# Layer 0's first and last blocks over three PSUM banks, its table cleared in pieces, and layer 3's output bias added by GpSimd

## The chip, the cores and the metric

The kernel runs on one core of one Trainium2 chip, in one launch. The metric is the device time in microseconds of that core. A profiled execution gives the trace; lines such as L187 are lines of the kernel before the change.

## The reference, cut to what matters

Four layers in a row turn `x` of 4 images, 128 channels and 48 x 48 pixels into an output of the same shape. All is float32.

- Layer 0, for each image: a layer norm over each pixel's channels, an input projection to 2 x 256 channels, a depthwise 3 x 3 convolution with silu, four selective scans (two directions by rows, two by columns) with 16 states over 2304 pixels, their sum, a norm over 256 channels, a gate, an output projection, and the image itself added.
- Layer 1: a deformable 3 x 3 convolution. A plain convolution of layer 0's output gives 27 offset channels; every output pixel then reads nine places of the image with bilinear weights. Pixels outside the image count as zero.
- Layer 2: eight linear-attention blocks, and then 64 experts that each take 8 tokens of every image.
- Layer 3: one causal attention with 4 heads of 32 channels over each image's 2304 tokens, and again 64 experts. Its output projection is `t = t + (out @ out_w.T + out_b)`, and the experts follow.

## The kernel before

**Layer 0** works image by image. Three steps matter here, and for images 1 to 3 (the first) and 0 to 2 (the last) they are slipped in among the scans of another image; only image 0's start and image 3's end stand alone.

- `before(im, j)`: six blocks of 384 pixels. A block is a list of ten steps: fetch `xb`, three transposes (L247), copy to `xt` (L251), statistics (L207 to L210, the last one a power on GpSimd), normalise (L214), three transposes back (L257), scale and shift into `xn` (L261) with a DMA of it to memory (L262), and two projections (L266), each copied into a padded image (L269).
- `convolve(d, r)`: 24 groups of nine matmuls over the padded image (L187), each emptied by ScalarE into `u_hw` (L294). Then silu (L302), and `prepare` for the first scan, whose first DMA writes `rows` (L372); the scans read `rows` back into `rB`, one DMA a step (L500).
- `post(im)` after an image's last scan: six blocks `after(im, j)` of 18 steps (fetch `yb`, `xn`, `xb`; transposes L634, copies L641, statistics, L214, transposes L648, L653, the gate L663 and L674, silu with its table load L677 and the reload L678, L681, projection L686, sum L691, transposes L697, L701 and the DMA L702 to `tok`), and then six blocks `offsets(im, j)`: two groups of nine matmuls (L187 with `l_woT`), L747, transposes L754, L760, and a DMA. After the last block four DMAs copy `tok` into `table` (L709). Layer 1 gathers from `table` (L949).

`merged(lists, lag)` puts lists of steps into one order, list i starting i x lag steps later. Image 0's blocks use lag 10, the last blocks lag 18; both are the length of a list, so that blocks follow one another. Every one of these steps takes its PSUM tile from the pool `pf`, which has one bank:

```
def psum(*shape):
    return pf.tile(list(shape), F32, name="pf", tag="pf")
```

PSUM's eight banks go to `ps` (two, for the scans' transposes), `pf` (one), `pu` (one, for `prepare`), `yp` (three) and `b0` (one).

`table` has a border of zeros. At the start GpSimd sets the whole of `y` (128 x 4608) to zero (L169) and ten DMAs copy it over the table (L173), 21.3 MB.

TensorE, ScalarE, VectorE and GpSimd take their instructions in program order (`manual_schedule`). The queue of SyncE (SP), which issues these DMAs, isn't in that list; its order is the scheduler's.

**Layer 3** runs scores (L2061), exponentials (L2069), masks on GpSimd (L2072) and weighted sums (L2090) block by block, while the row maxima of the next block (L2007, L2016, L2017) and the preparation of later ones (`prepare`: L1946, transposes L1958, projections L1964 and L1982) are slipped in between. `output` projects a finished block and adds it to the tokens `T`:

```
for g in range(G3):
    nc.tensor.matmul(pp[:, g, :], oT[:, bass.ts(g, P)], oT_w, start=True, stop=False)
    nc.tensor.matmul(pp[:, g, :], env.ones_row, o_b, start=False, stop=True)
dst = im.T[:, j * G3 : (j + 1) * G3, :]
nc.vector.tensor_add(dst, dst, pp)
```

These are L2041, L2042 and L2044; 24 blocks with three pairs each. `o_b` holds the bias with the values' bias folded in (L2145, L2146).

Of the kernel before, what the change touches and what calls it, by code (L numbers as in the profile page):

```python
# [23 lines left out]
P = 128  # L24
NB = 4
C = 128
# [73 lines left out]
]  # L100
NPI = len(PIECES)
TPC = CH // P
CT = 512
HBUF = 3
HB = BLK // 2
# [2 lines left out]
def _layer0(ctx, env, dr, io, table, offs):  # L108
# [16 lines left out]
    def load(name, shape):  # L125
        t = cp.tile(shape, F32, name=name)
        nc.sync.dma_start(t, io[name])
        return t

    def psum(*shape):  # L130
        return pf.tile(list(shape), F32, name="pf", tag="pf")

    ln_g = load("l0_ln_g", [P, 1])
# [27 lines left out]
    for pad in pads:  # L161
        nc.gpsimd.memset(pad, 0.0)


    u_hw = wp.tile([P, ND, L], F32, name="u_hw")
    u_wh = wp.tile([P, ND, L], F32, name="u_wh")
    y = wp.tile([P, ND, L], F32, name="y")
    zero = y.rearrange("p d f -> p (d f)")
    nc.gpsimd.memset(zero, 0.0)  # L169
    flat = table.rearrange("r c -> (r c)").rearrange("(p f) -> p f", p=P)  # L170
    for i in range(0, flat.shape[1], ND * L):
        w = min(ND * L, flat.shape[1] - i)
        nc.sync.dma_start(flat[:, i : i + w], zero[:, :w])  # L173


# [136 lines left out]

    def merged(lists, lag):

        out = []
        for t in range(max(i * lag + len(a) for i, a in enumerate(lists))):
            for i, a in enumerate(lists):
                if 0 <= t - i * lag < len(a):
                    out.append(a[t - i * lag])
        return out  # L320

    def chained(lists):
# [8 lines left out]
        return out  # L331

    def pre(im):
        items = merged([before(im, j) for j in range(NBLK)], 10)
        return items + chained([convolve(d, r) for r in range(L // HB) for d in range(ND)]) + [activate]

    class Piece:
# [279 lines left out]
    def after(im, j):  # L617

        cols = bass.ts(j, BLK)
        t = {}  # L620

        def fetch():
            t["yb"] = sp.tile([P, ND, BLK], F32, name="yb", bufs=1)
            nc.sync.dma_start(t["yb"], im.y[:, :, cols])
            t["xn"] = sp.tile([P, BLK], F32, name="xn")
            nc.sync.dma_start(t["xn"], im.xn[:, cols])
            t["xb"] = sp.tile([P, BLK], F32, name="xb")
            nc.sync.dma_start(t["xb"], io["x"][im.b][:, cols])

        def turn_y(g0, g1):  # L630
            t["pt"] = pt = psum(P, g1 - g0, DI)
            for g in range(g0, g1):
                for d in range(ND):
                    nc.tensor.transpose(  # L634
                        pt[:, g - g0, bass.ts(d, P)], t["yb"][:, d, bass.ts(g, P)], ident
                    )

        def turned(g0, g1):
            if g0 == 0:
                t["yt"] = sp.tile([P, G3, DI], F32, name="yt", bufs=1)  # L640
            nc.scalar.copy(t["yt"][:, g0:g1, :], t.pop("pt"))  # L641
            if g1 == G3:
                t["first"], t["second"] = standardise(t["yt"])

        def back_y(d):
            t["pt"] = pt = psum(P, BLK)
            for g in range(G3):
                nc.tensor.transpose(pt[:, bass.ts(g, P)], t["yt"][:, g, bass.ts(d, P)], ident)  # L648

        def normed(d):  # L650
            if d == 0:
                t["yn"] = sp.tile([P, ND, BLK], F32, name="yn", bufs=1)
            nc.scalar.activation(  # L653
                t["yn"][:, d, :],
                t.pop("pt"),
                AF.Identity,
                bias=ob[:, d : d + 1],
                scale=og[:, d : d + 1],
            )

        def gate(d):
            t["pz"] = psum(P, BLK)
            nc.tensor.matmul(  # L663
                t["pz"],
                ipT[:, DI + d * P : DI + (d + 1) * P],
                t["xn"],
                start=True,
                stop=True,
            )

        def gate_out(d):
            if d == 0:
                t["z"] = sp.tile([P, ND, BLK], F32, name="yt", bufs=1)
            nc.scalar.copy(t["z"][:, d, :], t.pop("pz"))  # L674

        def silu():
            nc.scalar.activation(t["z"], t["z"], AF.Silu)  # L677
            nc.scalar.preload_act_table_set(EXP_LN)  # L678

        def gated():  # L680
            nc.vector.tensor_mul(t["yn"], t["yn"], t["z"])  # L681
# [12 lines left out]
        def to_table():  # L694
            t["pt"] = pt = psum(P, G3, P)
            for g in range(G3):
                nc.tensor.transpose(pt[:, g, :], t["xb"][:, bass.ts(g, P)], ident)  # L697

        def out():
            xt = sp.tile([P, G3, C], F32, name="xt")  # L700
            nc.scalar.copy(xt, t.pop("pt"))  # L701
            nc.sync.dma_start(im.tok[cols, :].rearrange("(g p) c -> p g c", p=P), xt)  # L702
            if j == NBLK - 1:
                tb = table[im.b * TROWS : (im.b + 1) * TROWS, :].rearrange(
                    "(y x) (q c) -> y x q c", x=TW, c=C
                )
# [27 lines left out]

    def offsets(im, j):
        t = {}

        def third(i, n):
            if n == 0:
                t["pp"] = psum(NOFF, HB)  # L740
            taps(t["pp"], woT, pads[0], 2 * j + i, 3 * n, 3 * n + 3)

        def rows(i):
            if i == 0:
                t["fo"] = sp.tile([P, G3, DI], F32, name="yt", bufs=1)
                t["fo"] = t["fo"].rearrange("p g c -> p (g c)")[:NOFF, :BLK]
            nc.scalar.activation(  # L747
                t["fo"][:, bass.ts(i, HB)], t.pop("pp"), AF.Identity, bias=bo
            )

        def turn():
            t["pt"] = pt = psum(P, G3, NOFF)
# [21 lines left out]
        ]  # L774

    def post(im):
        return merged([after(im, j) for j in range(NBLK)], 18) + chained(
            [offsets(im, j) for j in range(NBLK)]
        )
# [21 lines left out]
                self.done += 1  # L801

    with tc.manual_schedule(engines=ORDERED):
        for s in pre(images[0]) + prepare(pieces[0], None):
            s()
        for g in range(3):
            do(row, g)
# [13 lines left out]
        for g in range(len(pieces) * NS + 2):  # L821
# [2 lines left out]
            if n == 0 and i + 1 < len(pieces):  # L824
                lanes["next"] = Lane(prepare(pieces[i + 1], pieces[i]), 3 * (NS - 3))
            if (p, n) == (0, 5) and b < NB:
                items = post(images[b - 1]) if b else []
                cols = [lambda d=d, j=j: columns(d, j) for j in range(NCH) for d in range(ND)]
                gap = len(items) // len(cols)
                for q, c in enumerate(cols):  # L830
# [33 lines left out]
            do(scan, g, 1)  # L864
        for d in range(ND):
            collect(pieces[-1], d)
        for s in post(images[-1]):
            s()

# [1003 lines left out]
def _layer3(ctx, env, io, T):  # L1873
# [26 lines left out]
    v_b = load("l3_v_b", [P, 1])  # L1900
    oT_w = load("l3_owT", [P, C])
    o_b = load("l3_ob", [1, C])
    later = load("l3_later", [P, P])

    spread = [cp.tile([P, G3, P], F32, name=f"spread{i}") for i in range(NP3)]
# [31 lines left out]
    def prepare(im, j):  # L1937
# [15 lines left out]
                )  # L1953

        def turn():
            pt = psum(P, BLK)
            for g in range(G3):
                nc.tensor.transpose(pt[:, bass.ts(g, P)], t["xn"][:, g, :], ident)  # L1958
# [78 lines left out]
    def output(im, j, oT):  # L2037
        def project():
            pp = psum(P, G3, C)
            for g in range(G3):  # L2040
                nc.tensor.matmul(pp[:, g, :], oT[:, bass.ts(g, P)], oT_w, start=True, stop=False)  # L2041
                nc.tensor.matmul(pp[:, g, :], env.ones_row, o_b, start=False, stop=True)  # L2042
            dst = im.T[:, j * G3 : (j + 1) * G3, :]
            nc.vector.tensor_add(dst, dst, pp)  # L2044

# [299 lines left out]
```

## Time and profile before

| what | us |
|---|---|
| median of 3 runs | 12765.19 (12760.49 to 12773.71) |
| profiled execution | 12769.64, of which the span is 12767.5 |
| image 0's six blocks, first transpose to first convolution | 10.44 to 102.58 |
| image 0's 24 convolution groups | 102.58 to 193.16, the start of the last L294 |
| first `rows` DMA of the scans | 204.46 |
| last image: `y` written, first transposes of its blocks | 5214.98, 5225.55 |
| last image: first offset convolution, copy of the last offsets | 5354.59, 5404.73 |
| layer 1's first gather | 5421.81 |
| layer 3: first statistics, start of the last sum into `T` | 11025.19, 12564.3 |

Over the whole span TensorE is busy for 10986.9 us (86%), VectorE 8483.4 (66%), ScalarE 6895.6 (54%), GpSimd 4394.0 (34%). In the timeline a line gives the start, the duration, the engine, the line of the kernel, the operation with what it writes and reads, and in brackets how long the engine sat idle before it and what ended that. A matmul in float32 is listed as two passes, so nine matmuls are x18.

### The profile page before, as it was taken

The numbers are of one execution on the slowest core, as the hardware profiler recorded it, in microseconds if no ns is written. First come the engines' busy times: TensorE is split into PE (matmuls) and PEld (weight loads), VectorE is DVE, ScalarE is ACT, GpSimd is POOL, SyncE is SP. The second block draws the span as 40 slices with busy tenths as digits, with TensorE's granted clock in tenths as the row PEclk, the third lists the DMA queues.
The fourth block names the chain that finished last, engine by engine and source line by source line (L and its number), as shares of the span: only waits on it lengthen the run. The fifth ranks groups of instructions, "written<-read, shape, count | busy, mean of one in ns | idle before, by whom it ended". The sixth has DMA issues, their size and how long they took to land.

```text
span 12767.5 us, 192717 instructions
## 1 busy us (share of the span) xinstructions
PE 10986.9 (86%) x71150; PEld 8409.7 (66%) x71150; DVE 8483.4 (66%) x15484; ACT 6895.6 (54%) x13189; POOL 4394.0 (34%) x4775
## 2 busy tenths in 40 slices
PE   6879778877887787588879999999999998799997
PEld 4667666766676666378757777777777776333333
DVE  4998889888988899444455656656566565445444
ACT  3777777777777677411125555555556565232222
POOL 1443333333333334166633333333333332100001
PEclk9999999999999999799979999999999999799998
DMA  2221222122222222266610000000000001200003
GB/s 103 67 70 65 76 79 69 65 77 79 69 65 75 82 66 68 65 174 174 177 44 2 4 3 4 4 2 4 2 4 4 1 1 43 84 6 7 7 8 124
DMA packets 307846, 677.50 MB, mean 53 GB/s; under 512 B 39108, under 2 KB 128984, under 8 KB 304864
## 3 DMA queue, kind: packets, MB, share of 16 engines
q1 hardware_dynamic: 254032, 493.49, 12.0%
q0 software_dynamic: 51840, 169.91, 4.6%
q8 instruction: 571, 9.36, 0.3%
q14 instruction: 363, 2.97, 0.1%
q10 hardware_dynamic: 1040, 1.77, 0.0%
HBM read 602.63 MB, written 71.85 MB: 53 GB/s over the span
## 4 chain that ended last, share of the span: by engine, by line
PE 43%; DVE 7%; ACT 3%; issue 1%; DMA 1%; POOL 1%; another core or an unknown queue 0%; SPq 0%; ACTq 0%; DVEq 0%; POOLq 0%
PE psum L1425 4%; PE pt L962 4%; PE psum L1417 4%; PE pc L1311 3%; PE psum L1361 3%; PE scT L2061 3%; PE sc L2007 3%; PE out L2090 3%; PE psum L1331 2%; PE psum L1171 2%; PE psum L1172 2%; PE psum L1105 2%; PE psum L1249 1%; PE psum L1350 1%; DVE mx L1334 1%
## 5 line engine op out<-in xcount | busy, mean ns | idle before, releaser
L565 ACT ACTIVATE hs<-ps,bct 128x256 f32<-128x256 f32 x4608 | 1858.3, 475 | 1171.1 <-PE ps L559 1121.1
L559 PE MATMUL ps<-ident,h 128*128 128x128 f32 x9216 | 1499.4, 295 | 776.2 <-DVE h L545 602.1
L559 PEld LDWEIGHTS ps<-ident,h 128*128 128x128 f32 x9216 | 1087.4, 149 | 1158.4 <-DVE h L545 708.5
L573 PE MATMUL yp<-ident,hs 128*128 128x128 f32 x9216 | 1409.1, 289 | 28.6 <-ACT ys L588 28.6
L505 ACT ACTIVATE dA<-delta,l_Al 128x768 f32<-128x768 f32 x1536 | 1388.4, 936 | 0.3
L512 POOL TENSOR_TENSOR h<-du,rB 128x512 f32<-128x512 f32 x768 | 1079.0, 1405 | 768.9 <-PE ps L559 691.0
L573 PEld LDWEIGHTS yp<-ident,hs 128*128 128x128 f32 x9216 | 1161.6, 151 | 83.0 <-ACT ys L588 57.7
L545 DVE TENSOR_TENSOR_SCAN h<-dA,h 128x256 f32<-128x256 f32 (+1 forms) x1024 | 1084.2, 1059 | 27.3
L545 DVE TENSOR_TENSOR_SCAN h<-dA,carry,h 128x768 f32<-128x768 f32 x512 | 1026.7, 2005 | 10.5 <-ACT dA L505 10.5
L1165 POOL TENSOR_TENSOR T<-T,bias 128x384 f32<-128x384 f32 x384 | 384.3, 1001 | 1558.5 <-DVE fn L1093 1518.3
L487 POOL TENSOR_SCALAR_AFFINE_SELECT dB<-bct 128x512 f32<-128x512 f32 x768 | 749.5, 976 | 379.2 <-PE b L519 236.3
L2069 ACT ACTIVATE pT<-scT 128x768 f32<-128x768 f32 (+2 forms) x504 | 378.1, 750 | 897.3 <-PE scT L2061 897.1
L519 PE MATMUL b<-dB,duT 128*128 128x128 f32 x6144 | 827.5, 278 | 0.8 <-ACT duT L445 0.8
L545 DVE TENSOR_TENSOR_SCAN h<-dA,carry,b 128x512 f32<-128x512 f32 x512 | 645.6, 1261 | 269.6 <-PE b L519 250.7
L962 PE MATMUL pt<-ident,gw 128*128 128x128 f32 x5184 | 677.1, 292 | 167.7 <-DVE gw L956 139.0
L949 POOL DMA_INDIRECT g<-table,idx x648 | 656.9, 1014 | 412.4 <-DVE gw L956 179.4
L962 PEld LDWEIGHTS pt<-ident,gw 128*128 128x128 f32 x5184 | 642.2, 205 | 197.3 <-DVE gw L956 133.5
L519 PEld LDWEIGHTS b<-dB,duT 128*128 128x128 f32 x6144 | 767.9, 196 | 2.4 <-POOL h L512 1.2
L956 DVE TENSOR_TENSOR gw<-g,wq 128x512 f32<-128x512 f32 x648 | 425.7, 692 | 494.1 <-PE pt L962 420.6
L552 POOL COPY carry<-h 128x2 f32<-128x2 f32 x512 | 97.9, 191 | 1784.4 <-DVE h L545 1714.5
L2017 DVE TENSOR_REDUCE mx<-sc 128x2 f32<-128x1024 f32 (+3 forms) x400 | 428.4, 1071 | 364.5 <-PE sc L2007 359.4
L516 DVE TENSOR_TENSOR h<-du,rB 128x512 f32<-128x512 f32 x768 | 629.3, 819 | 3.7 <-DMA rB<-rows 3.6
(345 smaller groups left out, 22964.7 us busy)
## 6 DMA issues: line engine op xcount, KB each, us to landing
rB<-rows SPq DMA_DIRECT2D x768, 384.0 KB
w<-f_w SPq DMA_DIRECT2D x64, 1024.0 KB
table<-y SPq DMA_DIRECT2D x9, 2304.0 KB
table<-tok SPq DMA_DIRECT2D x16, 1152.0 KB
g<-table,idx POOLq DMA_INDIRECT x648
xb<-x SPq DMA_DIRECT2D x48, 192.0 KB
xn<-xn SPq DMA_DIRECT2D x48, 192.0 KB
yd<-y SPq DMA_DIRECT2D x4, 2304.0 KB
```

The lines of the kernel that those rows point to most:

```text
L487: nc.gpsimd.affine_select(out=x.dB[n], in_=x.bc[:, m0 : m0 + CT // P, n : n + 1].to_broadcast([P, CT // P, P]), pattern=[[0, CT // P], [1, ...
L505: nc.scalar.activation(dA, x.delta[:, d, :], AF.Exp, scale=A[:, d, x.k, n : n + 1])
L512: nc.gpsimd.tensor_mul(h[:, 1, own], x.du[:, 1, own], x.rB[n][:, own])
L516: nc.vector.tensor_mul(x.h[n][:, :, own], x.du[:, :, own], b)
L519: nc.tensor.matmul(b0[:, bass.ts(m, P)], x.duT[:, m, :], x.dB[n][:, m, :], start=True, stop=True,)
L545: nc.vector.tensor_tensor_scan(h, da, b, initial=first, op0=ALU.mult, op1=ALU.add)
L559: nc.tensor.transpose(tt[:, m, bass.ts(d, P)], x.h[n][:, d, bass.ts(2 * q + m, P)], ident)
L565: nc.scalar.activation(hs, tt[:, m, :], AF.Copy, scale=x.bc[:, 2 * q + m, NS + n : NS + n + 1])
L573: nc.tensor.matmul(yp[:, q, (2 * d + m) * P : (2 * d + m + 1) * P], hs[:, bass.ts(d, P)], ident, is_transpose=True, start=n == 0 and m == ...
L949: nc.gpsimd.indirect_dma_start(out=g, out_offset=None, in_=table, in_offset=bass.IndirectOffsetOnAxis(ap=idx[:, j : j + 1], axis=0),)
L962: nc.tensor.matmul(pt[:, t - t0, :], gw[:, q, :], ident, start=q == 0, stop=q == 3)
L1417: nc.tensor.matmul(pg, y.w["w1"][:, bass.ts(f, P)], t["uT"], start=True, stop=True)
```

## The change

The pieces are independent of one another.

1. While `banks` is filled, `psum` hands out three banks in turn, `pf` and the two of `ps`. It is filled for image 0's start and for the last image's end. Image 0's blocks then start every 3 steps instead of every 10.
2. The last image's blocks start every 6 steps instead of every 18, its offset blocks start at step 23 and then every 9 steps, and take their PSUM tile from `pu`. Their SBUF tiles come from buffers of the scans (`h`, `dA0`, `dA1`, `rB`, `xd`).
3. A tile of zeros of 128 x 256 takes the place of the zeroed `y`; 163 DMAs of 128 KB (the last one smaller) take the place of ten. Their calls stand in the list of steps that goes along with image 0's scans, between the six transposing copies of `columns`.
4. In layer 3 the bias row is spread over 128 partitions once (one matmul, one copy), GpSimd adds it to a block's tokens when the block is prepared, after it was normalised, and the 72 ones-row matmuls go.

```diff
+ZW = 256
...
+    banks = []
+
     def psum(*shape):
+        if banks:
+            banks.append(banks.pop(0))
+            pool, name = banks[-1]
+            return pool.tile(list(shape), F32, name=name, tag=name)
         return pf.tile(list(shape), F32, name="pf", tag="pf")
...
-    zero = y.rearrange("p d f -> p (d f)")
+    zero = cp.tile([P, ZW], F32, name="zero")
     nc.gpsimd.memset(zero, 0.0)
     flat = table.rearrange("r c -> (r c)").rearrange("(p f) -> p f", p=P)
-    for i in range(0, flat.shape[1], ND * L):
-        w = min(ND * L, flat.shape[1] - i)
+
+    def clear(i):
+        w = min(ZW, flat.shape[1] - i)
         nc.sync.dma_start(flat[:, i : i + w], zero[:, :w])
...
     def merged(lists, lag):
+        starts = lag if isinstance(lag, list) else [i * lag for i in range(len(lists))]
...
     def pre(im):
-        items = merged([before(im, j) for j in range(NBLK)], 10)
+        items = merged([before(im, j) for j in range(NBLK)], 3 if banks else 10)
...
         def fetch():
-            t["yb"] = sp.tile([P, ND, BLK], F32, name="yb", bufs=1)
+            if banks:
+                t["yb"] = sp.tile([P, ND, CH], F32, name="h", bufs=HBUF)[:, :, :BLK]
+                t["xn"] = sp.tile([P, CH], F32, name="dA0")[:, :BLK]
+                t["xb"] = sp.tile([P, CH], F32, name="rB", bufs=3)[:, :BLK]
+            else:
+                t["yb"] = sp.tile([P, ND, BLK], F32, name="yb", bufs=1)
...
-                t["yn"] = sp.tile([P, ND, BLK], F32, name="yn", bufs=1)
+                if banks:
+                    t["yn"] = sp.tile([P, CH], F32, name="dA1")
...
-                t["z"] = sp.tile([P, ND, BLK], F32, name="yt", bufs=1)
+                t["z"] = sp.tile([P, ND, BLK], F32, name="yb" if banks else "yt", bufs=1)
...
     def offsets(im, j):
+        def own(*shape):
+            return pu.tile(list(shape), F32, name="pu", tag="pu") if banks else psum(*shape)
...
     def post(im):
+        if banks:
+            lists = [f(im, j) for f in (after, offsets) for j in range(NBLK)]
+            starts = [6 * j for j in range(NBLK)]
+            starts += [9 * j + 23 for j in range(NBLK)]
+            return merged(lists, starts)
...
     with tc.manual_schedule(engines=ORDERED):
-        for s in pre(images[0]) + prepare(pieces[0], None):
+        free = [(pf, "pf"), (ps, "ps"), (ps, "ps")]
+        banks += free
+        for s in pre(images[0]):
+            s()
+        del banks[:]
+        for s in prepare(pieces[0], None):
             s()
...
-                items = post(images[b - 1]) if b else []
+                if b:
+                    items = post(images[b - 1])
+                else:
+                    items = [lambda i=i: clear(i) for i in range(0, flat.shape[1], ZW)]
...
+        banks += free
         for s in post(images[-1]):
             s()
...
+    bias = cp.tile([P, 1, C], F32, name="bias")
...
         def turn():
+            own = im.T[:, j * G3 : (j + 1) * G3, :]
+            nc.gpsimd.tensor_add(own, own, bias.to_broadcast([P, G3, C]))
             pt = psum(P, BLK)
...
-                nc.tensor.matmul(pp[:, g, :], oT[:, bass.ts(g, P)], oT_w, start=True, stop=False)
-                nc.tensor.matmul(pp[:, g, :], env.ones_row, o_b, start=False, stop=True)
+                nc.tensor.matmul(pp[:, g, :], oT[:, bass.ts(g, P)], oT_w, start=True, stop=True)
...
+        pr = psum(P, C)
+        nc.tensor.matmul(pr, env.ones_row, o_b, start=True, stop=True)
+        nc.scalar.copy(bias[:, 0, :], pr)
         run(normed(images[0]) + prepare(images[0], 0))
```

More of the change, by code (lines that the diff above doesn't have):

```diff
@@ L313, in merged @@
     def merged(lists, lag):
+        starts = lag if isinstance(lag, list) else [i * lag for i in range(len(lists))]
         out = []
[L316 to L319, printed above, removed]
+        for t in range(max(i + len(a) for i, a in zip(starts, lists))):
+            for i, a in zip(starts, lists):
+                if 0 <= t - i < len(a):
+                    out.append(a[t - i])
         return out
@@ L622, in fetch @@
         def fetch():
-            t["yb"] = sp.tile([P, ND, BLK], F32, name="yb", bufs=1)
+            if banks:
[4 more added lines that the diff above has]
+                t["yb"] = sp.tile([P, ND, BLK], F32, name="yb", bufs=1)
+                t["xn"] = sp.tile([P, BLK], F32, name="xn")
+                t["xb"] = sp.tile([P, BLK], F32, name="xb")
             nc.sync.dma_start(t["yb"], im.y[:, :, cols])
-            t["xn"] = sp.tile([P, BLK], F32, name="xn")
             nc.sync.dma_start(t["xn"], im.xn[:, cols])
-            t["xb"] = sp.tile([P, BLK], F32, name="xb")
             nc.sync.dma_start(t["xb"], io["x"][im.b][:, cols])
@@ L651, in normed @@
             if d == 0:
-                t["yn"] = sp.tile([P, ND, BLK], F32, name="yn", bufs=1)
+                if banks:
+                    t["yn"] = sp.tile([P, CH], F32, name="dA1")
+                    t["yn"] = t["yn"].rearrange("p (d f) -> p d f", d=ND)
+                else:
+                    t["yn"] = sp.tile([P, ND, BLK], F32, name="yn", bufs=1)
             nc.scalar.activation(
@@ L736, in offsets @@
         t = {}
+        def own(*shape):
+            return pu.tile(list(shape), F32, name="pu", tag="pu") if banks else psum(*shape)
         def third(i, n):
             if n == 0:
-                t["pp"] = psum(NOFF, HB)
+                t["pp"] = own(NOFF, HB)
             taps(t["pp"], woT, pads[0], 2 * j + i, 3 * n, 3 * n + 3)
@@ L744, in rows @@
             if i == 0:
-                t["fo"] = sp.tile([P, G3, DI], F32, name="yt", bufs=1)
-                t["fo"] = t["fo"].rearrange("p g c -> p (g c)")[:NOFF, :BLK]
+                if banks:
+                    t["fo"] = sp.tile([NR + 2 * NS, CH], F32, name="xd", bufs=1)
+                else:
+                    t["fo"] = sp.tile([P, G3, DI], F32, name="yt", bufs=1)
+                    t["fo"] = t["fo"].rearrange("p g c -> p (g c)")
+                t["fo"] = t["fo"][:NOFF, :BLK]
             nc.scalar.activation(
@@ L751, in turn @@
         def turn():
-            t["pt"] = pt = psum(P, G3, NOFF)
+            t["pt"] = pt = own(P, G3, NOFF)
             for g in range(G3):
@@ L776, in post @@
     def post(im):
+        if banks:
+            lists = [f(im, j) for f in (after, offsets) for j in range(NBLK)]
+            starts = [6 * j for j in range(NBLK)]
+            starts += [9 * j + 23 for j in range(NBLK)]
+            return merged(lists, starts)
         return merged([after(im, j) for j in range(NBLK)], 18) + chained(
@@ L826, in _layer0 @@
             if (p, n) == (0, 5) and b < NB:
-                items = post(images[b - 1]) if b else []
+                if b:
+                    items = post(images[b - 1])
+                else:
+                    items = [lambda i=i: clear(i) for i in range(0, flat.shape[1], ZW)]
                 cols = [lambda d=d, j=j: columns(d, j) for j in range(NCH) for d in range(ND)]
```

## The prediction

> **What bounds the kernel now.** I read the page's forty slices first, then busy time by stage, then the timeline of the stages that the change touches, and last the waits.
>
> ```profile
> PEclk9999999999999999799979999999999999799998
> ```
>
> The clock granted to TensorE has three 7s. The first, slice 17, is layer 0's end. Now the stages: image 0's blocks, its convolution, the last image's blocks, its offset convolution, and layer 3 after its start.
>
> ```profile
> core 0: us, PE busy (x) PEld busy (x) DVE busy (x) ACT busy (x) POOL busy (x), PEclk, DMA share, GB/s
> 10.00:102.00 92.00, 30.62 (x60) 12.31 (x60) 22.47 (x87) 6.90 (x12) 5.13 (x6) 1.00 0.63 258
> 103.00:193.00 90.00, 78.16 (x432) 71.22 (x431) 0.00 (x0) 9.69 (x23) 0.00 (x0) 1.00 0.00 1
> 5225.00:5354.00 129.00, 65.00 (x138) 27.85 (x138) 27.82 (x72) 42.45 (x60) 8.16 (x12) 0.51 0.13 35
> 5355.00:5405.00 50.00, 41.68 (x234) 24.01 (x232) 1.47 (x6) 4.95 (x12) 0.00 (x0) 0.95 0.36 103
> 11140.00:12565.00 1425.00, 1309.00 (x6206) 509.22 (x6205) 672.98 (x1122) 431.10 (x618) 65.79 (x139) 0.93 0.03 7
> ```
>
> In the two block stages no engine is busy for more than half the time: they are chains through one PSUM bank, and the latency of the chain ends last. Layer 3 is TensorE's: 1309 of 1425 us. The timeline shows the front's two losses, a stall and a pause for each convolution:
>
> ```profile
> 37.33 0.91 PE L257 MATMUL pf<-ident,xt 128*128 128x128 f32 x3 [3.62 <-DVE xt L214]
> 64.72 0.67 ACT L261 ACTIVATE xn<-pf,l_ln_b,l_ln_g 128x384 f32<-128x384 f32 x1 [30.46 <-DMA xn<-xn]
> ...
> 112.13 3.19 PE L187 MATMUL pf<-pad,diag 128*128 128x192 f32 x18 [0.51 <-ACT u_hw L294]
> 115.36 0.42 ACT L294 ACTIVATE u_hw<-pf,l_cb 128x192 f32<-128x192 f32 x1 [3.28 <-PE pf L187]
> 115.83 3.19 PE L187 MATMUL pf<-pad,diag 128*128 128x192 f32 x18 [0.51 <-ACT u_hw L294]
> ```
>
> L261 of the third block needs a buffer whose write to `xn` stands behind 21 MB of zeros for the table; after the transposes it would have started at 38.3, so 26.4 us are lost. And every convolution waits 0.51 us for the one bank to be emptied. In layer 3 the output projection alternates weights with the bias row:
>
> ```profile
> 11639.99 0.49 PE L2041 MATMUL ps<-l_owT,sums 128*128 128x128 f32 x2
> 11640.41 0.48 PE L2042 MATMUL ps<-l_ob,ones_row 1*128 1x128 f32 x2
> 11640.83 0.49 PE L2041 MATMUL ps<-l_owT,sums 128*128 128x128 f32 x2
> 11642.60 0.55 DVE L2044 TENSOR_TENSOR T<-T,ps 128x384 f32<-128x384 f32 x1 [1.26 <-PE ps L2042]
> ```
>
> From start to start a pair takes 0.42 us, the bias as much as the projection.
>
> **The change, part by part.** The sum is made against the profiled execution, 12769.64 us (span 12767.5); it lies 4.45 above the median 12765.19, inside the runs' own spread of 13 us.
>
> *Image 0's blocks.* Before, six blocks of 10.8 us (10.44 to 22.11) and the 26.4 us stall put the first convolution at 102.6. Changed, a block starts every 3 steps and three banks rotate. TensorE's queue then repeats: projection, next block's transposes, second projection, previous block's back-transposes. At the durations of this stage (L266 1.65, L247 0.90, L257 0.91) that is 5.1 us, and once in each round TensorE waits for L261 (0.67 and the two hand-overs, 0.8). The round is 5.9 us. VectorE needs less: three pairs of statistics 1.5, two small steps with GpSimd's power 1.3, L214 0.9, two pad copies 1.1, hand-overs, near 5.3. The first block's back-transposes end at 16.7 as now (VectorE's 18 `diag` products until 12.9 still go ahead), the second's at 22.6, the sixth's at 22.6 + 4 x 5.9 = 46.2, and L261 with two projections brings 51. Gain 51.5. If fetches and the two `xn` buffers stretch the round to 8 us it is 43; if TensorE warms up and VectorE's 5.3 sets the round, 54.
>
> *Its convolution.* 24 groups back to back: 24 x 3.19 and 2.1 for the first, cold one (5.27 at 102.58) are 78.7, against 90.6. Gain 12. L294 (0.42) is hidden under the next group's 3.19. Convolutions end at 130, and the first row transfer of the scans is due 11.3 us later (193.2 to 204.5 now), at 141.
>
> *The clears.* The text puts them among the scans, but SP's queue is not kept in program order: in the built changed kernel all 163 stand before the first `rows` write, 29 between the fetches and `xn` writes of image 0, then 134 in a row. So they don't do what their place says; what hides them is the convolution. From the last `xn` write, 47, to 141 there are 94 us, 0.70 us for each of 134. No 128x256 store is in the trace. The nearest row is the load of `l_opT`, also 128x256: issued at 6.31, the next at 6.79, so 0.48 and 64 us in all, done at 111. The other bound is the spacing of the old clears, 13.40 us for 10: 1.34 each, 180 us, done at 227, and 86 us lost. I take the first, since `table<-tok` with packets of 512 B moved 339 GB/s (5360 to 5364), which is 0.39 us for 128 KB. The scans lose nothing then, and 0 us is charged. On a rule: DMA: Bandwidth & Descriptors, section Bandwidth, of the Trainium skill asks for batches of 1 MiB and lists 138 GB/s at 64 KB. By that figure 21.3 MB would take an estimated 154 us and cost some 20 us of the gain; no run yet shows which holds.
>
> *The last image's blocks and offsets.* The yd round trip (5215.0 to 5225.5) stays. Before: six blocks of 21.6 us in turn, then six offset blocks of 7.98, until 5405.1: 179.6 us. Changed: a block starts every 6 steps of 18, offsets start at step 23 and then every 9 steps in their own bank, 77 steps in all. ScalarE's part of a round is 42.45 / 6 = 7.1 us, its loop of silu with two table loads 3.4, L653 twice, L641 twice, then L674, L701, L674, each behind a TensorE step. At half clock TensorE needs 65.0 / 6 = 10.8 and the loop comes to 12.5; at full clock (L663's form takes 0.91 in layer 3 instead of 1.65) TensorE needs 6.1 and the loop 9.0. TensorE, over 85% busy in the cold loop, should warm up: it did at 5360, within 6 us of such work. Steps 0 to 5 are 6 us (5225.55 to 5231.6), 6 to 11 are 9.5, 12 to 23 are 21; in 24 to 47 offsets share TensorE, 6.6 us a block (two groups of 3.11 and 0.37) of which two thirds, 4.4, fall in six steps: 10.5, with waits 11.3 a round, 45; 48 to 77 leave three offset blocks of 7.98 and a rest, 25.5. Sum 107. Gain 72.5; 50 with rounds of 12.5 and 14; 84 with 9 and 10. What could be late next is the table: its four copies take 10.67 us to issue and landed within 20 us of 5356.9; the last offset blocks (25 us) and layer 1's start (5405.2 to the first gather at 5421.8) cover them. Uncovered they would cost up to 20.
>
> *Layer 3's bias.* 72 matmuls go, three in each of 24 projections: 24 x 3 x 0.415 = 30 us of TensorE. VectorE waited 42.3 us in 23 of the 24 for just these, 1.84 on average, so L2044 comes earlier by nearly all of it; some comes out of waits for VectorE's reductions (11640.11 to 11641.34), so I take 26, and 8 to 34 as ends. GpSimd gets 24 sums of 128x384; the same form, L1165 in layer 2, takes 1001 ns, 24 us on an engine busy for 65.79 of 1425. Queued behind a sum are the masks L2072, 1 us late; TensorE uses a masked tile three units later, over 5 us. The new matmul and copy at layer 3's start fall into TensorE's idle time until 11036. The price may be VectorE's:
>
> ```profile
> 5194.82 1.33 POOL L512 TENSOR_TENSOR h<-du,rB 128x512 f32<-128x512 f32 x1 [1.91 <-PE ps L559]
> 5194.94 2.83 DVE L545 TENSOR_TENSOR_SCAN h<-dA,carry,h 128x768 f32<-128x768 f32 x1
> ...
> 5200.23 1.81 DVE L545 TENSOR_TENSOR_SCAN h<-dA,carry,h 128x768 f32<-128x768 f32 x1
> ...
> 10334.86 0.99 POOL L1165 TENSOR_TENSOR T<-T,bias 128x384 f32<-128x384 f32 x1
> ...
> 10335.50 0.51 DVE L1334 TENSOR_REDUCE mx<-psum 128x8 f32<-128x352 f32 x1
> ```
>
> A scan that began inside a GpSimd product took 1.02 us more; a reduction from PSUM beside the bias sum took its usual 0.5. Layer 3's VectorE mostly reads PSUM (L2016, L2017, L2028, L2044), so I charge nothing; charged in full it would be 24 x 1.0. SBUF — State Buffer, section Who interferes with whom, of the Trainium skill says why: VectorE and GpSimd share one port pair, locked for a whole instruction, which a VectorE instruction with two SBUF inputs needs and a reduction doesn't. It speaks against the edit only for L2117 and L1946, an estimated few us.
>
> Sum: 51.5 + 12 + 72.5 + 26 = 162. 12769.6 - 162 = 12607.6, and 4.45 less for the median: about 12604.
>
> **The rivals.** *Layer 3 gains nothing* (VectorE held by the sums, or the freed time turned into waits for its reductions): 162 - 26, 12630. For it: TensorE already waits 107 us for L2017. Against: the 42.3 us above. *The tail stays at half clock*: 6 + 10 + 25 + 4 x 19 + 25 = 142 (19: TensorE's 10.8 and two thirds of two cold groups of 5.72) instead of 107, so 12639. For it: 0.51 through 129 us. Against: that was at half occupancy. *The clears cost 1.34 us each*: 12690. *Slower than before*: the clears go out one at a time, each at a load's whole way (`xb` issued at 7.66, used at 10.44: 2.8 us). 134 x 2.8 = 375 from 47, the first `rows` at 422 instead of 141, 281 lost, 12885. It decides from (94 + 162) / 134 = 1.9 us a clear. Against it: `l_Al`, issued at 4.42, was used at 6.37, and four more loads were issued in between, one every 0.47 us.
>
> **How the numbers follow.** Forecast 0.62, layer 3 without gain 0.15, cold tail 0.13, 1.34 us clears 0.05, the slower case 0.04, no difference 0.01. The ends of the parts (43 + 12, 50, 8 and 54 + 13, 84, 34) give 113 to 185, which holds the first three cases: 12580 to 12653, rounded out to 12578 and 12655. About 0.2%, 25 us, is what a measurement of this kernel tells from no change: faster 0.95, same 0.01, slower 0.04.
>
> **What would show it.** The first L187 of the changed kernel near 51 and the first `rows` near 141, with the clears landed before; convolution groups without a gap; from the first `yb` to the last offsets about 107 us, clock near 1.0 after the first 20; layer 3 about 26 us shorter, VectorE's L2017 not longer. A `rows` write waiting behind clears, or a tail over 130, makes it wrong.

## The result: 231 us faster, 67 us below the forecast

The changed kernel takes 12537.1 us (median of four runs, 12530.7 to 12545.3), the kernel before 12768.1 in the same set: ratio 0.9819, 95% interval 0.9807 to 0.9831. In a second set the ratio was 0.9804 (0.9789 to 0.9819). The forecast was 12604, with a range from 12578: the direction was right, the gain was 231 us instead of 162, and the time fell below the range.

The profiled execution of the changed kernel has a span of 12543.6 us, that of the kernel before 12767.5: 223.9 less. Landmarks of the two traces, in us:

| landmark | before | after | gain up to here |
|---|---|---|---|
| first convolution matmul | 102.6 | 40.2 | 62.4 |
| first `rows` write of the scans | 204.5 | 121.9 | 82.6 |
| write of yd (scans done) | 5215.0 | 5128.7 | 86.3 |
| last transposes of the offsets (L754, now L781) | 5404.3 | 5237.8 | 166.5 |
| first gather of layer 1 | 5421.8 | 5255.8 | 166.0 |
| layer 3's first statistics | 11025.2 | 10884.7 | 140.5 |
| layer 3's last output sum (L2044, now L2088) | 12564.3 | 12338.2 | 226.1 |

So the front gave 82.6, the tail 80.2, layer 3 gave 85.6; 25.5 seem lost between the first gather and layer 3, in code that is the same in both kernels.

In the page's clock line slice 17, layer 0's end, is an 8 instead of a 7:

```profile
PEclk9999999999999999899979999999999999799998
```

The stages that answer to those of the prediction (image 0's blocks, its convolution, the last image's blocks and offsets together, layer 3 after its start). The columns are as there: busy time and count of each engine, granted clock, DMA share, GB/s.

```profile
10.00:40.00 30.00, 20.01 (x60) 11.15 (x61) 18.75 (x74) 6.89 (x12) 5.12 (x6) 0.89 0.59 192
40.00:110.50 70.50, 70.50 (x434) 70.13 (x432) 0.85 (x2) 9.67 (x23) 0.00 (x0) 1.00 0.75 249
5139.00:5246.00 107.00, 79.10 (x372) 44.29 (x372) 30.62 (x86) 48.08 (x74) 8.14 (x12) 0.87 0.34 97
11000.00:12339.00 1339.00, 1219.75 (x6058) 466.32 (x6058) 670.56 (x1118) 430.07 (x618) 85.73 (x159) 0.98 0.03 7
```

Image 0's blocks went from 92 us to 30 with the same 60 matmul records, and the convolution keeps TensorE busy for all of its 70.5 us. The tail's TensorE has a mean clock of 0.87 over blocks and offsets together; before, it was 0.63 over the same two stages (0.51 in the blocks, 0.95 in the offsets). In layer 3 TensorE's busy time fell from 1309 to 1220, by 89 us (87 from the first output sum to the last), though the removed matmuls were priced at 30; its clock rose from 0.93 to 0.98, and VectorE's busy time is what it was (673 and 671).

In the timeline of the changed kernel, the start of a block's statistics, the convolution, and SP's queue around the last clears:

```profile
20.45 0.28 DVE L216 BATCH_NORM_STATS2 s<-xt 128x6 f32<-128x128 f32 x1
...
24.70 0.28 DVE L216 BATCH_NORM_STATS2 s<-xt 128x6 f32<-128x128 f32 x1
...
40.17 3.09 PE L196 MATMUL pf<-pad,diag 128*128 128x192 f32 x18
43.10 6.02 PE L196 MATMUL ps<-pad,diag 128*128 128x192 f32 x36
...
104.16 5.84 SPq L182 DMA_DIRECT2D table<-zero  x9
...
121.90 0.33 SPq L383 DMA_DIRECT2D rows<-xd  x1
```

In the middle a block starts every 4.25 us (4.3 on average over the six); then comes a convolution group every 2.93 us without a gap, and the last clear is issued 12 us before the first `rows` write. Now layer 3's output projection after, and behind it the same place in the kernel before:

```profile
11460.92 0.94 PE L2086 MATMUL ps<-l_owT,sums 128*128 128x128 f32 x6
11462.78 0.91 PE L2009 MATMUL ps<-xT,l_wqk 128*128 128x384 f32 x2 [0.92 <-DVE T L2088]
...
11464.42 0.92 PE L2105 MATMUL scT<-q,k 64*128 64x384 f32 x4
```

```profile
11507.96 0.49 PE L2041 MATMUL ps<-l_owT,sums 128*128 128x128 f32 x2
...
11510.04 0.48 PE L2042 MATMUL ps<-l_ob,ones_row 1*128 1x128 f32 x2
11511.17 1.65 PE L1964 MATMUL ps<-xT,l_wqk 128*128 128x384 f32 x2 [0.65 <-DVE T L2044]
...
11513.37 1.65 PE L2061 MATMUL scT<-q,k 64*128 64x384 f32 x4
```

An output took 2.56 us (11507.96 to the end of the sixth matmul at 11510.52), and takes 0.94. After it, before the change, the same `scT` product takes 1.65 instead of 0.92: TensorE is at half clock. The clock records of the trace show 22 such spells between the first and the last output, 178 us in all, each a multiple of 3.4 us (3.4 to 17.1, but for the last, which begins ahead of the last output and runs on behind it); after the change 10 spells and 61 us, all around the changes of image, where TensorE waits mostly for VectorE, and the last one. TensorE: Matmul & The Clock Gate, section Part 1 (The HAM clock gate), of the Trainium skill gives a free-running window of 3.4 us in which activity is watched; the lengths of the spells agree. What brings the spells on is what the experiments had to find.

### The profile page after: what moved, and what is told of

It is laid out like the page before. It is cut to its first block, busy times and chain, and to the rows that moved or that the text cites. A ratio compares the mean times of both kernels' runs of the same rounds, so it can differ in the third digit from the quotient of the medians.

```text
span 12543.6 us, 192625 instructions
## 1 busy us (share of the span) xinstructions
PE 10872.6 (87%) x71008; PEld 8365.3 (67%) x71008; DVE 8487.3 (68%) x15484; ACT 6888.6 (55%) x13190; POOL 4409.7 (35%) x4799
## 4 chain that ended last, share of the span: by engine, by line
PE 43%; DVE 7%; ACT 3%; issue 1%; DMA 1%; POOL 1%; another core or an unknown queue 0%; SPq 0%; ACTq 0%; DVEq 0%; POOLq 0%
PE psum L1466 4%; PE pt L1003 4%; PE psum L1458 4%; PE pc L1352 3%; PE psum L1402 3%; PE scT L2105 3%; PE sc L2052 3%; PE out L2134 3%; PE psum L1372 2%; PE psum L1212 2%; PE psum L1213 2%; PE psum L1146 2%; PE psum L1290 1%; PE psum L1391 1%; DVE mx L1375 1%
```

## The experiments

Theory: matmuls with one row of weights, half of every output's time, count little as TensorE work, so that the clock falls behind many outputs. Rivals: the longer output and the pause behind it do this, whatever the rows; or only the 30 us of matmuls went and the rest was chance. The table has, for each profile, layer 3 from its first statistics to its last sum, the part of it from the first output sum to the last ("body"), an output's length, and the half clock in the body (without its first and last 3 us). The last column counts the spells that have output matmuls, 0.3 us or more of them, in the 3.4 us ahead of them.

| kernel | layer 3 | body | one output | half clock | spells behind outputs |
|---|---|---|---|---|---|
| before / before_again | 1539.1 / 1515.2 | 1423.2 / 1401.7 | 2.56 | 178 / 126 | 12 / 8 |
| l3_undone | 1525.5 | 1412.1 | 2.56 | 153 | 9 |
| l3_rows32 | 1494.8 | 1379.9 | 2.56 | 73 | 4 |
| l3_wide | 1476.0 | 1365.4 | 1.78 | 86 | 2 |
| l3_rows128 | 1462.9 | 1351.7 | 1.61 | 59 | 0 |
| l3_no_bias | 1459.8 | 1346.2 | 0.94 | 80 | 0 |
| after / after_again | 1453.5 / 1450.2 | 1340.1 / 1342.9 | 0.94 | 61 / 67 | 0 / 0 |

The five profiles whose edits leave the changed kernel's layer 3 alone (front_old, clears_old, zw128, tail_old, better_rows) have 1451.2 to 1456.7 there, and no spell behind an output but two in clears_old.

l3_undone, l3_rows32, l3_rows128 and l3_no_bias ran on a chip on which layer 1, from its first gather on, takes 913 us instead of 1014 to 1038 in the other profiles (the kernel before 12673.9 there), so times are compared as ratios to the kernel before in the same set.

**l3_undone: layer 0's parts alone.**

```
-            nc.gpsimd.tensor_add(own, own, bias.to_broadcast([P, G3, C]))
...
-   matmul(pp[:, g, :], oT[:, bass.ts(g, P)], oT_w, start=True, stop=True)
+   matmul(pp[:, g, :], oT[:, bass.ts(g, P)], oT_w, start=True, stop=False)
+   matmul(pp[:, g, :], env.ones_row, o_b, start=False, stop=True)
```

> The changed kernel with layer 3's part undone: 72 one-row bias matmuls again, no sums on GpSimd. Theory (one-row matmuls count little as TensorE work for the clock gate, so that every output projection, half of it such matmuls, is followed by a spell at half clock): layer 3, from its first statistics to its last output sum, takes 1539 us again instead of 1453.5, some 170 to 180 us of it at half clock between its first and last 100 us instead of 58, and the kernel 12537 + 86 = 12623. Rival (only the 30 us of matmul time went, and the rest of the 86 us was chance): layer 3 1484, kernel 12567. Second rival (layer 0's new order helped layer 3): 1453 to 1484.

12504.9 us, 0.9868 (0.9851 to 0.9884). Against 0.9819 and 0.9804 of the changed kernel, layer 3's part is worth 62 to 81 us of 12674 by these ratios. The profile puts it where the theory does:

```profile
10878.60:12290.70 1412.10, 1296.36 (x6202) 503.75 (x6202) 671.82 (x1120) 430.97 (x618) 65.08 (x139) 0.94 0.03 7
```

Clock 0.94, TensorE busy for 1296 us. Layer 3 takes 1525.5 us, where 1539 was expected, with 153 us of half clock instead of 170 to 180, inside what the two profiles of the kernel before have. That only the matmuls' 30 us went, or that layer 0's order helped, is out.

**l3_rows128 and l3_rows32: the same number of matmuls, more rows.** Shown against l3_undone:

```
+    even = cp.tile([128, P], F32, name="even")   # or 32
+    nc.gpsimd.memset(even, 1.0 / 128)
...
-   matmul(pp[:, g, :], env.ones_row, o_b, start=False, stop=True)
+   matmul(pp[:, g, :], even, bias[:128, 0, :], start=False, stop=True)
```

> As l3_undone, but each bias matmul has 128 rows (weights 1/128, the bias spread over all partitions): the same number of matmuls, passes and waits, no sums on GpSimd. Theory (rows count): no spells after the output projections, layer 3 1453.5 + 30 = 1484, half clock about 60 us, kernel 12567. Rival (the projection that ends 1.25 us later makes TensorE wait for VectorE, and the pause drops the clock, whatever the rows): 1539, half clock 175, kernel 12623.

> The same with 32 rows. Theory in proportion to rows: a quarter of the work counts, so spells in part: layer 3 1500 to 1530, kernel 12585 to 12615. Theory with a threshold between 1 and 32 rows: 1484 and 12567, as with 128. Rival (pause): 1539 and 12623.

128 rows: 12445.6 us, 0.9820 (0.9803 to 0.9836), the changed kernel's time with the bias still on TensorE. 32 rows: 12489.5, 0.9857 (0.9841 to 0.9873). From one output of 128 rows, and the matmul behind it, then from one of 32:

```profile
11351.28 0.39 PE L2087 MATMUL ps<-bias,even 128*128 128x128 f32 x2
11351.51 0.39 PE L2086 MATMUL ps<-l_owT,sums 128*128 128x128 f32 x2
...
11353.21 0.91 PE L2009 MATMUL ps<-xT,l_wqk 128*128 128x384 f32 x2 [0.65 <-DVE T L2089]
```

```profile
11353.96 0.48 PE L2087 MATMUL ps<-bias,even 32*128 32x128 f32 x2
11354.37 0.49 PE L2086 MATMUL ps<-l_owT,sums 128*128 128x128 f32 x2
11354.79 0.48 PE L2087 MATMUL ps<-bias,even 32*128 32x128 f32 x2
```

Two things show here, the pace and the clock. From start to start a matmul takes 0.22 to 0.23 us where its neighbours have 128 rows too, and 0.42 where they alternate with 32 rows, the same as with one; the 128-row projections between are slowed as well. The clock over the body, with 128 rows and with 32:

```profile
10884.70:12236.40 1351.70, 1236.25 (x6202) 483.07 (x6202) 671.37 (x1119) 430.28 (x618) 65.09 (x139) 0.98 0.03 7
```

```profile
10879.80:12259.70 1379.90, 1264.32 (x6203) 492.42 (x6202) 671.70 (x1119) 430.26 (x618) 64.82 (x138) 0.97 0.03 7
```

The pause for VectorE behind an output is 0.65 us with 128 rows as with one, and 0.92 behind the output of the changed kernel shown above, yet no spell follows an output with 128 rows or in the changed kernel. That refutes the pause.

The runs don't say whether the few rows do it or the slow alternation that few rows bring. With 32 rows an output is as long as with one (2.56), and the profile has 73 us of half clock, within the 59 to 80 of the kernels without matmuls of few rows, where the three profiles with one-row matmuls between the projections have 126 to 178. But it is the profile of the fastest of four runs: 12466.3 us at a granted clock of 0.954 over the whole run, where the other three took 12486.7 to 12503.3 at 0.951 to 0.952. l3_undone's four runs have 0.950 to 0.951, l3_rows128's 0.953 to 0.955. By the medians l3_rows32 is 15 us below l3_undone and 44 above l3_rows128, of which the longer outputs are 24 x 0.95 = 23. So most of its runs lose clock too; that 32 rows are enough is not shown.

I had expected 1484 for 128 rows; it is 1463, since I priced a 128-row matmul at 0.415.

**l3_wide: one wide one-row matmul ahead of the projections.** Shown against l3_undone:

```
+   matmul(pp, env.ones_row, o_b3, start=True, stop=False)     # 384 columns
    for g in range(G3):
-       matmul(pp[:, g, :], oT[...], oT_w, start=True, stop=False)
-       matmul(pp[:, g, :], env.ones_row, o_b, start=False, stop=True)
+       matmul(pp[:, g, :], oT[...], oT_w, start=False, stop=g == G3 - 1)
```

> Layer 3's bias on TensorE as one matmul with one row of weights and 384 columns ahead of the three projections, in place of three between them; no sums on GpSimd; layer 0 as in the changed kernel. From the first output sum to the last, layer 3 takes 1340 us in the changed kernel, 1412 with three one-row matmuls in turn with the projections, 1380 with 32 rows, 1352 with 128. Theory (a projection next to a matmul with another number of rows takes 0.42 us instead of 0.22, and the half clock comes from 2.5 us of such slow work): an output takes 0.94 + 0.4 to 0.6, so 1350 to 1355, half clock 60 to 80 us. Rival (any one-row matmul in the output brings the spells): 1380 or more, half clock over 120.

12575.4 us, 0.9841 (0.9824 to 0.9857); body 1365, 10 to 15 above my number; the wide matmul takes 0.84 (2 x 0.42), not 0.4 to 0.6, which is 6 to 11 of it. The three projections side by side take 0.94 again. Half clock is 86, with 2 spells behind outputs: 0.84 us of one-row work ahead of an output costs the clock little, 1.25 us among 2.56 costs it much. Both readings, few rows and slow alternation, allow for that.

**l3_no_bias: without GpSimd's sums.**

```
-            nc.gpsimd.tensor_add(own, own, bias.to_broadcast([P, G3, C]))
```

> The changed kernel without the 24 sums on GpSimd: the bias is left out of the output. Theory (the sums cost nothing, GpSimd is idle and VectorE isn't held): layer 3 1453 within 3, kernel 12537 within 8. Rival (VectorE held by them or masks late): up to 24 us less, 12513.

12429.3 us, 0.9802 (0.9786 to 0.9819): the changed kernel's ratio within the intervals. Its body is 1346 against 1340 and 1343 with the sums. They cost nothing that shows, as the prediction took it.

**front_old and clears_old: the two halves of the front.** The first puts image 0 back into one bank, blocks in turn, and keeps the small clears; the second keeps the three banks and puts back the ten large clears from `y`.

```
-        banks += free
         for s in pre(images[0]):
             s()
-        del banks[:]
```

> The changed kernel with image 0's blocks and convolution in turn in one PSUM bank, as in the kernel before; the 163 small clears and all else stay changed. Expected from the stages: no 26 us stall, six blocks of 10.8 us, first convolution matmul at 76 (40.2 in the changed kernel, 102.6 before), 90.6 us of convolution, first row transfer of the scans at 178 (121.9 and 204.5). That is 56 us more than the changed kernel, 0.9863 of the kernel before. Rival (the three banks also cleared the stall, the small clears alone don't): first convolution near 100, ratio 0.988.

```
-    zero = cp.tile([P, ZW], F32, name="zero")
+    zero = y.rearrange("p d f -> p (d f)")
     nc.gpsimd.memset(zero, 0.0)
+    for i in range(0, flat.shape[1], ND * L):  # one DMA of 128 x 4608 each
...
```

> The changed kernel with the table cleared as before (10 large DMAs from the zeroed y, ahead in SP's queue); three banks stay. Expected: the third block's normalization waits for its xn buffer until 64.7 as before, the three blocks left take 20 us, first convolution at 85, convolution groups back to back, first row transfer at 167: 45 us more than the changed kernel, 0.9854 of the kernel before. Rival (with three banks the stall doesn't end last): first convolution at 40 to 45, ratio 0.982.

Both came close to what was expected. front_old: 12603.7 us, 0.9860 (0.9844 to 0.9877), first convolution at 74.9, first `rows` write at 176.5. clears_old: 12588.2, 0.9849 (0.9832 to 0.9865), 80.3 (85 expected) and 162.1. So the small clears alone move `rows` by 28.0 (204.5 to 176.5), the banks alone by 42.4, and both together by 82.6: while the third block waits for its `xn` write until 65, the banks have nothing to overlap. In what they give, these two pieces of the change are not independent. clears_old also shows what `y`'s zeroing did to VectorE:

```profile
5.52 3.94 POOL L177 MEMSET y<- 128x4608 f32 x1
...
6.79 6.14 DVE L166 TENSOR_SCALAR diag<-ident,l_cw 128x128 f32<-128x128 f32 x18
```

The 18 products take 3.61 us in the changed kernel, where GpSimd zeroes only 128x256 (0.31 us), and the first statistics start at 11.70 instead of 12.85.

**zw128: clears half as wide.**

```
-ZW = 256
+ZW = 128
```

> The changed kernel with clears half as wide (128x128, 326 of them instead of 163). They took 0.53 us each at 128x256 and were issued by 109.6, with the first row transfer of the scans due at 121.9. If the bytes set the rate: 0.27 us each, done at the same time, 0.982 of the kernel before. If the DMA or its 128 rows set the rate (0.53 us each whatever the width): issued by 195, the row transfers late by some 75 us, ratio 0.988. In between if part of both.

12545.6 us, 0.9814 (0.9797 to 0.9830): no loss, but not because bytes set the rate.

```profile
98.81 22.84 SPq L182 DMA_DIRECT2D table<-zero  x45
123.89 0.32 SPq L383 DMA_DIRECT2D rows<-xd  x1
124.25 0.90 SPq L182 DMA_DIRECT2D table<-zero  x2
```

45 clears of 64 KB in 22.84 us are 0.51 each, hardly less than those of 128 KB (95 in a row in 50.10, 0.53): between these two sizes the rate goes by the DMA of 128 rows, not by bytes. The last one was issued at 240.6. Yet the first `rows` write went out at 123.9, since in this build SP's queue has the row transfers between the clears, and they hold no scan up. My 75 us rested on a queue with all clears in front. What the changed kernel's clears would cost if they outlasted the convolution was therefore not measured.

**tail_old: the last image's blocks and offsets in turn.**

```
-        banks += free
         for s in post(images[-1]):
```

> The changed kernel with the last image's blocks and offsets as before (blocks every 18 steps in one bank, then the offset blocks in turn). From the write of yd to the last offset copy 189.7 us instead of 116.7, so 73 us more than the changed kernel: 0.9877 of the kernel before. Rival (layer 1's start waits for the table in any case): 60 us or less, 0.9866.

12619.3 us, 0.9876 (0.9860 to 0.9891). The last offset transposes start at 5318.9, 81.0 after the changed kernel's, and the first gather at 5335.8, 80 later. In all three kernels the first gather follows these transposes by 17 to 18 us, and in the changed kernel's profile it waits for ScalarE's work on the offsets (L975), so the table, whose four copies are issued from 5215.1 to 5222.1 there, is not what it waits for.

**after_again and before_again: both kernels unedited in one set.**

> The changed kernel once more, unedited, as the measure on the chip of this set. 0.982 of the kernel before; first gather of layer 1 at 5256, layer 3 from its first statistics to its last sum 1453 us. From the first gather to layer 3's first statistics its profile took 5629 us, and that of the kernel before 5603: theory (chance, the code between is the same): the two differ by less than 10 us in this set. Rival (the change costs 25 us there): 20 to 30 us again.

> The kernel before once more, unedited, for its profile: time ratio 1.000; from the first gather to layer 3's first statistics within 10 us of the changed kernel's in this set if that difference was chance, 20 to 30 us less if the change costs it.

after_again 12534.1 us, 0.9804 (0.9789 to 0.9819); before_again 1.0003 (0.9993 to 1.0013). From the first gather to layer 3's first statistics: 5626.3 and 5625.7. The 25.5 us were chance, and most of it in the first profile of the kernel before: of the other nine profiles with a layer 1 of this length, eight have 5623 to 5633 there, and the ninth is that of the next experiment, which edits this code. Layer 3 took 1515.2 and 1450.2 in this pair, so its part is worth 65 here and 86 in the first pair; with one-row matmuls between the projections its half clock differs from execution to execution (126, 153, 178 us).

**better_rows: the other one-row matmuls with 128 rows.** In layer 1 (72) and layer 2 (96); all else as in the changed kernel.

```
-   matmul(out, env.ones_row, shift[:1, :], start=False, stop=True)
+   matmul(out, ident, shift, start=False, stop=True)
-   matmul(out, ones[:, :n], eps_row, start=False, stop=False)
+   matmul(out, ident[:, :n], eps_row, start=False, stop=False)  # eps_row on 128 partitions
```

> The changed kernel with two more one-row matmuls turned into matmuls with 128 rows (the identity as weights, the row spread over all partitions): layer 1's shift, 72 of them, and layer 2's small constant in the context, 96. Same numbers of matmuls, same sums. Theory (a matmul whose number of rows differs from its neighbours' takes 0.42 us instead of 0.22 to 0.23): 168 x 0.19 = 32 us less where TensorE is the bound, 12 to 32 us in all, 0.9800 of the kernel before. Rival (hidden under gathers in layer 1 and waits in layer 2): 0.982.

12508.7 us (12504.6 to 12516.8), 0.9786 (0.9773 to 0.9799), beside 12534.1 (12525.3 to 12537.5) of the changed kernel in the same set: 25 us less, and the lowest ratio of all. Layer 1 gained nothing (1032.6 against 1030.7), so there it was hidden. From layer 1's end to layer 3 it took 4563.6 instead of 4595.6:

```profile
8007.08 0.40 PE L1348 MATMUL pc<-wv,xb 128*128 128x136 f32 x2
8007.31 0.40 PE L1351 MATMUL pc<-l_eps,ident 128*128 128x136 f32 x2
8007.54 4.33 PE L1353 MATMUL pc<-v,dk 128*128 128x136 f32 x36
```

The first two lines take 0.46 us up to the third's start; with one row they took 0.75, and the group behind them 0.11 more: 0.40 x 96 = 38 us of TensorE, of which 32 show. From the first of layer 2's 96 matmuls to the last there are 41 us of half clock in both kernels, so a single one-row matmul among full ones costs time but not the clock.

## Why the prediction was off, step by step

*Layer 3's bias: the step that failed.* "24 x 3 x 0.415 = 30 us of TensorE. ... I take 26, and 8 to 34 as ends." Measured: 86 in the first pair, 65 in the second, 62 to 81 by the ratios. That the removed matmuls come off TensorE's time was right; the term was mis-sized, in two ways. First, a matmul taken out of an alternating pair frees its neighbour too: an output fell from 2.56 to 0.94, so 24 x 1.62 = 39 us, not 30. I read "the bias as much as the projection" in the pair and didn't compare the 0.42 with projections side by side. Second, the clock, which the sum put at nothing. Half clock fell by 117 us in the first pair and 59 in the second, which at full work is worth half, 59 and 30. Together that is at most 98 and 69, of which 83 and 59 show in the bodies: TensorE's busy time fell by 87 and 63, since it isn't busy for all of the half clock, and its idle time rose by 4. The 0.93 stood in the first view that I showed, and I took it for granted instead of asking what came before each spell. The rival that layer 3 gains nothing was wrong, and the price of a VectorE held by the sums is nothing that shows. What makes the clock fall is narrowed to the one-row matmuls in turn with the projections; whether by their rows or by the slow pace stays open.

*Image 0's blocks.* First convolution forecast at 51, measured at 40.2: 10.9 more gain. The rounds are 4.25 us instead of 5.9. The three durations that I added (1.65, 0.90, 0.91) came from a stage with idle gaps, where TensorE was at half clock by these durations (the 1.00 in the prediction's row means only that the trace has no clock record before 106 us); overlapped, the second projection takes 0.81 at 22.4 and 26.1 us, and the clock of the stage is 0.89. VectorE, put at 5.3, goes through its steps for a block in 4.25. The zeroing of `y` that held VectorE is another 1.2: I left the 18 products "until 12.9" as they were.

*Its convolution.* 2.93 a group, not 3.19: the 3.19 runs to the end of a group's last matmul, and back to back the next group starts ahead of that end (40.17 + 3.09 is 43.26, the next start is 43.10). From start to start a group is 0.26 shorter than I took it: 0.26 x 24 = 6.2 us. The 2.1 for a cold first group fell away as well (3.09). Blocks and convolution together gave 82.6 instead of 63.5, which lies above their own ends too (54 + 13 = 67).

*The clears.* Right: all 163 in front of `rows`, 0.53 us each against the forecast's 0.48, the last one issued 12 us ahead of `rows` instead of 30, and 0 us lost. 128 KB in 0.53 us are 247 GB/s. The 138 GB/s that DMA: Bandwidth & Descriptors, section Bandwidth, of the Trainium skill lists at 64 KB, measured on loads, is near what zw128's clears of 64 KB make (0.51 us, 128 GB/s); carried over to 128 KB it was too low, and the 20 us that it would have cost did not appear. The 1.34 and 2.8 us rivals are out.

*The tail.* 80.2 against 72.5, inside its own ends of 50 and 84. From the first transposes of `yb` (5139.5) to the end of the last offset transposes 99 us instead of 107, at a clock of 0.59 in the first 20 us and 0.97 after; the cold tail was wrong, and tail_old confirms the size.

The three mis-sized terms all err to the same side, mostly by the same habit: durations taken from the stage as it was, with its cold clock, the ends of its groups and its slowed neighbours. All rivals lay on the slow side, so the range had no room for it. 162 + 19.1 (front and convolution) + 7.7 (tail) + 60 or 39 (layer 3), with 4 from the scans, is 253 for the first pair of profiles and 232 for the second. Less the chance 25 in the first it is 228 and 232 (with the first pair's front and tail in both), where the spans differ by 223.9 and 226.5.

Three slips of the working changed nothing: 12607.6 less 4.45 is 12603; the 10.8 us of a block before is that of the second on (22.11 to 32.80), while 10.44 to 22.11 is 11.7; and in the last image's blocks TensorE was busy for just over half the time (65 of 129 us).

## What to carry to other kernels

Ask of a matmul that is removed or moved what its neighbours cost without it: from start to start, in a place of the trace where they already stand side by side. A bias from a ones row between other matmuls was not cheap on TensorE here, although it moves few bytes; on an idle engine it cost nothing that shows, and as a matmul with 128 rows, the row spread over the partitions, less than half as much (an output of 1.61 instead of 2.56, beside 0.94 without). A mean clock below 1 in a stage with a busy TensorE is a term of its own: look at what runs in the few us ahead of each spell.

## What the runs showed of the hardware

- Matmuls that alternate between 128 rows of weights and 1 or 32 take 0.42 us each from start to start for 128 columns, two of 128 rows 0.22. Only the number of rows differed.
- One-row matmuls that alternate with projections and fill half of 2.56 us are often followed by half clock, for 3.4 to 17.1 us: 8 to 12 spells for 24 outputs. With 128 rows in their place, or none, the four such profiles of the table have no spell behind an output, though the pause is the same 0.65 us or longer. Whether a spell follows differs between outputs and executions. 32 rows keep the slow pace; how much of the clock they cost was not settled.
- SP sends a DMA of 128 rows every 0.51 us at 512 B a row and every 0.53 at 1 KB.
- A GpSimd memset of 128x4608 made 18 VectorE products of 128x128 take 6.05 to 6.14 us instead of 3.61; GpSimd's sums of 128x384 in layer 3 cost VectorE nothing that shows: 670 us of busy time with and without them.
